# Cutting the last 4 MB store of a subject-conditioned residual matmul into six stores by partitions

## The chip, the core and the metric

One core of a Trainium2 chip runs the program. The metric is the time of one execution in device microseconds. Three timed runs of the kernel before gave 326.16, 326.69 and 326.79 us; their median, 326.69 us, is the time before.

## The reference

```python
# x: (128, 128, 1024) f32, itok: (128,) int32 in 0..7, weights: (8, 128, 128) f32
w = weights[itok]                              # one 128x128 matrix for each batch row
out = x + jnp.einsum('bct,bcd->bdt', x, w)     # (128, 128, 1024) f32
```

Each of 128 samples (128 channels by 1024 time steps, 512 KB) is multiplied by the matrix of its subject and added to itself. 67.1 MB are read and 67.1 MB are written.

## The kernel before

The identity is added to the weights on the chip, so that one matmul gives `x + w x`. The work runs over `NT` = 32 tiles of `Q` = 4 samples (2 MB). The first `FIRST` = 4 tiles have a layout of their own. A later tile lies in SBUF so that a partition holds two neighbouring channels of two samples, and the output lies in the same way.

- ACT issues all loads of `x` (`load`, `load_rows`) on its own DMA queue and copies half of each product from PSUM into `x_out` (`swap`). After each tile it writes one element of `mark`; that copy raises `s_added[1]`.
- DVE copies the other half (`copy`) and builds the next weights (`place`). The first instruction of `place` raises `s_added[0]`.
- SP issues all stores (`store`) on its DMA queue, in the order of the list `stores`: 20 stores of one tile (2 MB), then 6 stores of two tiles (`PAIR`, 4 MB). Before each it waits for `s_added[0]` and `s_added[1]`. A store reads `x_out` on 128 partitions. In a store of 4 MB a partition holds 32 KB, which goes to four places of 8 KB in `out`.
- PE multiplies in a loop, GpSimd only passes on semaphores (`s_room`, `s_ready`).

All of this stands in one block in which the waits are written by hand (`tc.tile_critical()`, L298). Only the last store is outside: `last = store(*stores[-1])` (L453) comes after that block, so SP issues it when all engines have reached the block's end. The end of the program waits for it. ACT meanwhile waits at the program's end (L449, L484) for the completion semaphores `s_out` of the stores before it.

`x_out` has eight slots, and the last store lies in two of them that no later tile needs.

## Time and profile before

| what | value |
|---|---|
| time, median of 3 runs | 326.69 us (326.16 to 326.79) |
| the profiled execution's own time | 328.88 us |
| its span, first to last instruction | 327.1 us |
| PE, DVE, ACT busy | 76%, 44%, 37% of the span |
| queue of the loads (q10), queue of the stores (q1) | 48.8%, 48.1% of 16 DMA engines |
| moved | 134.81 MB, mean 412 GB/s |

The page's line "DMA" gives the mean busy share of the 16 DMA engines in 40 slices of the span, in tenths; "GB/s" is what they moved. In a DMA view of a window, "under 512 B" counts the small packets, among which are those that raise a completion semaphore (4 bytes each). The view of a source line gives the least, median and longest duration in ns, and the first and last start in us. "SPq" and "ACTq" are the instruction queues of these engines, whose waits and DMA issues are not counted as busy.

### The profile page before, as it was taken

What the parts mean: (1) busy time and instruction counts of PE and PEld (TensorE: products, weight loads), DVE (VectorE), ACT (ScalarE), POOL (GpSimd) and SP (SyncE); (2) the same over time, 40 slices, a digit from 0 to 9 for tenths busy, and PEclk for the clock granted to TensorE, in tenths of its full rate; (3) what the DMA queues carried; (4) which work ended last, traced back from release to release, by engine and by line L of the source; (5) the groups of instructions that cost most, each with busy time, mean ns of one, the idle gap of its engine ahead of it and who ended that gap; (6) DMA issues with size and microseconds to landing.
All of it is one profiled execution on the core that took longest, in us unless ns stands there. A gap on an engine that the chain in (4) does not pass through costs nothing. (4 is left out here: it accounts for less than half of the span.)

```text
span 327.1 us, 5320 instructions
## 1 busy us (share of the span) xinstructions
PE 250.2 (76%) x1870; PEld 93.7 (29%) x1870; DVE 143.4 (44%) x207; ACT 120.4 (37%) x142; POOL 1.8 (1%) x8
## 2 busy tenths in 40 slices
PE   7899888888888888888395676978679808999200
PEld 3344333333333333333132222333223303333000
DVE  2386835555555555555513555135441530555500
ACT  0200005555555555555523555235451530555500
POOL 2000000000000000000000000000000000000000
PEclk9999979999999999999789999899898976999955
DMA  7999999999999999999999999999999999999890
GB/s 230 423 429 427 422 441 423 426 437 419 435 439 421 437 435 425 425 445 421 431 421 439 425 420 435 429 431 459 419 425 431 433 417 425 421 437 437 385 393 20
DMA packets 8247, 134.81 MB, mean 412 GB/s; under 512 B 1585, under 2 KB 2610, under 8 KB 2610
## 3 DMA queue, kind: packets, MB, share of 16 engines
q10 hardware_dynamic: 4496, 67.64, 48.8%
q1 hardware_dynamic: 3746, 67.11, 48.1%
q8 instruction: 2, 0.03, 0.0%
q14 instruction: 3, 0.02, 0.0%
HBM read 67.63 MB, written 67.11 MB: 412 GB/s over the span
## 5 line engine op out<-in xcount | busy, mean ns | idle before, releaser
L249 PE MATMUL ps<-x_in,w 64*64 64x512 f32 x1792 | 213.6, 620 | 51.1 <-PEq L240 47.4
L278 ACT COPY x_out<-ps 64x1024 f32 (+1 forms) x112 | 112.8, 1007 | 173.8 <-ACTq L293 171.7
L266 DVE COPY x_out<-ps 128x1024 f32 x56 | 68.6, 1225 | 145.7 <-DVEq L437 145.7
L249 PEld LDWEIGHTS ps<-x_in,w 64*64 64x64 f32 x1792 | 78.5, 138 | 186.2 <-issue 186.2
L197 DVE TENSOR_TENSOR w<-w_all,same 64x256 f32<-64x256 f32 x120 | 50.4, 420 | 2.6
L225 PE MATMUL ps<-x_in,w 128*128 x64 | 28.0, 597 | 1.0 <-PEq L222 1.0
L272 DVE COPY x_out<-ps 128x2048 f32<-128x2048 f32 x8 | 18.3, 2292 | 5.0 <-DVEq L426 5.0
L225 PEld LDWEIGHTS ps<-x_in,w 128*128 128x128 f32 x64 | 11.9, 190 | 17.1 <-issue 17.1
L209 DVE TENSOR_TENSOR w<-x_out 128x128 f32<-128x128 f32 x16 | 3.6, 285 | 6.4 <-DMA x_out<-in_L_cond_weights_dram 3.7
L312 PE MATMUL ps<-x_out 128*128 128x512 f32 x6 | 4.9, 982 | 1.7 <-DVE x_out L309 1.7
L284 ACT ACT_TABLE_LOAD x1 | 1.3, 1283 | 12.1 <-issue 12.1
L296 ACT COPY mark<-same 1x1 f32 (+1 forms) x28 | 5.3, 190 | 0.7
L356 PE MATMUL ps<-x_out 128*128 128x512 f32 x8 | 3.7, 601 | 0.3 <-DMA x_out<-in_L_cond_weights_dram 0.3
L312 PEld LDWEIGHTS ps<-x_out 128*128 128x128 f32 x6 | 1.8, 328 | 3.7 <-issue 2.1
L284 DVE COPY w_all<-ps 128x1024 f32<-128x1024 f32 x1 | 1.2, 1225 | 2.7 <-PE ps L356 2.7
L356 PEld LDWEIGHTS ps<-x_out 128*128 128x128 f32 x8 | 1.4, 189 | 2.7 <-issue 2.7
L284 ACT COPY w_all<-ps 128x1024 f32<-128x1024 f32 x1 | 1.0, 1012 | 0.0
L309 DVE MEMSET x_out<- 128x512 f32 x1 | 0.5, 485 | 1.0 <-SPq L298 1.0
L380 DVE TENSOR_SCALAR x_out<-x_out 1x128 int32<-1x128 int32 x1 | 0.4, 388 | 0.6 <-DMA x_out<-in_itok_B_dram 0.6
L337 POOL TENSOR_SCALAR_AFFINE_SELECT same<-same 128x256 f32<-128x256 f32 x1 | 0.5, 527 | 0.1
L325 POOL TENSOR_SCALAR_AFFINE_SELECT x_out<-x_out 128x256 f32<-128x256 f32 x1 | 0.4, 425 | 0.0
L337 POOL TENSOR_SCALAR_AFFINE_SELECT same<-x_out 128x256 f32<-128x256 f32 x1 | 0.4, 419 | 0.0
(9 smaller groups left out, 1.4 us busy)
## 6 DMA issues: line engine op xcount, KB each, us to landing
x_in<-in_x_dram ACTq DMA_DIRECT2D x56, 1024.0 KB, 12.5
out_dram<-x_out SPq DMA_DIRECT2D x20, 2048.0 KB, 56.7
out_dram<-x_out SPq DMA_DIRECT2D x6, 4096.0 KB, 46.7
x_in<-in_x_dram ACTq DMA_DIRECT2D x16, 512.0 KB, 10.0
x_out<-in_L_cond_weights_dram ACTq DMA_DIRECT2D x1, 512.0 KB, 5.2
x_out<-in_itok_B_dram SPq DMA_DIRECT2D x1, 0.5 KB
```

The source lines that it names most:

```text
L197: nc.vector.tensor_tensor(ws[u][p][h * A : (h + 1) * A], w_all[h * A : (h + 1) * A, bass.ds(subject[p * H + h], 1), :], same[h * A : (h + ...
L209: nc.vector.tensor_tensor(ws[u][q // H][:, :, q % H * D : (q % H + 1) * D], w_nat[:, bass.ds(subject[q], 1), :], eye, ALU.add,)
L225: mm = nc.tensor.matmul(ps[p][:, bank], ws[u][p][:, 0, h * D : (h + 1) * D], x_in[:, bass.ds(slot * (Q * T) + ((p * H + h) * T + t), N)], ...
L249: mm = nc.tensor.matmul(ps[p][cols, bank], ws[i % 2][p][rows, 0, r * D + e * A : r * D + (e + 1) * A], x_in[rows, at : at + N], start=r == ...
L266: return nc.vector.tensor_copy(x_out[:, bass.ds(at, T)], ps[0][:, banks].rearrange("d b n -> d (b n)"))
L272: return nc.vector.tensor_copy(x_out[:, at : at + SIZE], ps[p].rearrange("d b n -> d (b n)"))
L278: return nc.scalar.copy(x_out[h * A : (h + 1) * A, bass.ds(at + SIZE, T)], ps[1][(1 - h) * A : (2 - h) * A, banks].rearrange("d b n -> d ( ...
L284: engine(w_all.rearrange("c s (r e a) -> c r s e a", r=R, e=R)[:, r], ps[1][:, r * R : (r + 1) * R].rearrange("c g (s a e) -> c (g s) e a" ...
L296: nc.scalar.copy(mark[:, bass.ds(slot, 1)], same[:1, 0, :1]).then_inc(s_added[1], 1)
L312: nc.tensor.matmul(ps[P - 1][:, BANKS - 1], zeros[:, :D], zeros, start=True, stop=True)
L337: nc.gpsimd.affine_select(same[:, 0, :], same[:, 0, :] if h else zeros[:, : R * D], [[2 * C, R], [-2 * C, R], [-1, A]], ALU.not_equal, 1.0 ...
L356: nc.tensor.matmul(ps[1][:, r * R + g], pick[:, r], w_raw[:, g * N : (g + 1) * N], start=True, stop=True,).then_inc(s_picked, 1)
```

## The change

The last store is issued as six stores, by partitions: 0 to 111, 112 to 119, 120 to 123, 124 and 125, 126, and 127. The first five are moved into the block, behind the hand-written waits on `s_added`, and share the new semaphore `s_tail`. Only the store of partition 127 stays behind the block. ACT waits at the end for `s_tail` as well.

```diff
+TAIL = (0, 112, 120, 124, 126, 127, 128)
...
+    s_tail = tc.alloc_semaphore("s_tail")
...
-    def store(i, n):
+    def store(i, n, first=0, last=None):
         at = i % OUT * P * SIZE
+        part = slice(first, C if last is None else last)
...
-            there,
-            x_out[:, at : at + n * P * SIZE].rearrange("a (o f) -> a o f", o=1),
+            there[part],
+            x_out[part, at : at + n * P * SIZE].rearrange("a (o f) -> a o f", o=1),
...
             store(i, n).then_inc(s_out[i % OUT], DMA)
+        i, n = stores[-1]
+        nc.sync.wait_ge(s_added[0], i + n)
+        nc.sync.wait_ge(s_added[1], i + n - FIRST)
+        for first, last in zip(TAIL[:-2], TAIL[1:-1]):
+            store(i, n, first, last).then_inc(s_tail, DMA)
...
                 nc.scalar.wait_ge(s_out[i % OUT], stored[i][1])
-    last = store(*stores[-1])
+        nc.scalar.wait_ge(s_tail, DMA * (len(TAIL) - 2))
+    last = store(*stores[-1], TAIL[-2], TAIL[-1])
```

On SP, the end of the program before the change: the five earlier stores of 4 MB, the end of the block (three rows), the wait for all engines, and the last store (`out_dram` is the output, `128x4x2048` are 128 partitions of four runs of 2048 elements).

```order
L65 DMA out_dram<-x_out 128x4x2048 [waits s_added1,s_added0] x5
L291 UNCONDITIONAL_BRANCH
L298 UNCONDITIONAL_BRANCH
L298 NO_OP [waits SP_49,DVE_sequencer_49,PE_sequencer_49,SP_sequencer_49,Activation_sequencer_49,Pool_sequencer_49]
L484 UNCONDITIONAL_BRANCH
L65 DMA out_dram<-x_out 128x4x2048
L484 UNCONDITIONAL_BRANCH
```

The same place on SP after the change.

```order
L67 DMA out_dram<-x_out 128x4x2048 [waits s_added1,s_added0] x5
L67 DMA out_dram<-x_out 112x4x2048 [waits s_added1,s_added0]
L67 DMA out_dram<-x_out 8x4x2048
L67 DMA out_dram<-x_out 4x4x2048
L67 DMA out_dram<-x_out 2x4x2048
L67 DMA out_dram<-x_out 1x4x2048
L295 UNCONDITIONAL_BRANCH
L302 UNCONDITIONAL_BRANCH
L302 NO_OP [waits SP_49,DVE_sequencer_49,PE_sequencer_49,SP_sequencer_49,Activation_sequencer_49,Pool_sequencer_49]
L494 UNCONDITIONAL_BRANCH
L67 DMA out_dram<-x_out 1x4x2048
L494 UNCONDITIONAL_BRANCH
```

Five stores now stand ahead of the wait for all engines, and one partition is stored behind it.

On ACT, the end of the program before the change: the last copy of `mark`, then the rows that only wait (`s_out0`, `s_out2`, `s_out4` are earlier stores of 4 MB, the names with 49 are engines at the end of a block).

```order
L296 COPY mark<-same 1x1
L291 UNCONDITIONAL_BRANCH
L298 UNCONDITIONAL_BRANCH
L449 NO_OP [waits SP_49,SP_sequencer_49]
L484 UNCONDITIONAL_BRANCH [waits Activation_sequencer_49,Pool_sequencer_49,PE_sequencer_49,s_out4,DVE_sequencer_49,s_out2,SP_sequencer_49,s_out0,SP_49]
L449 NO_OP [waits Activation_49,Activation_sequencer_49]
L484 UNCONDITIONAL_BRANCH
```

And after it.

```order
L300 COPY mark<-same 1x1
L295 UNCONDITIONAL_BRANCH
L302 UNCONDITIONAL_BRANCH
L458 NO_OP [waits SP_49,SP_sequencer_49]
L494 UNCONDITIONAL_BRANCH [waits Pool_sequencer_49,Activation_sequencer_49,s_tail,PE_sequencer_49,s_out4,DVE_sequencer_49,s_out2,SP_sequencer_49,s_out0,SP_49]
L458 NO_OP [waits Activation_49,Activation_sequencer_49]
L494 UNCONDITIONAL_BRANCH
```

ACT's wait now takes in `s_tail`, which the first five parts of the last store raise; its other waits are the same.

## The prediction

> **What bounds the kernel now.** I read the page's DMA parts first.

> ```profile
> DMA  7999999999999999999999999999999999999890
> q10 hardware_dynamic: 4496, 67.64, 48.8%
> q1 hardware_dynamic: 3746, 67.11, 48.1%
> out_dram<-x_out SPq DMA_DIRECT2D x6, 4096.0 KB, 46.7
> ```

> The two queues together keep 16 DMA engines busy for 97% of the span: the kernel is bound by its transfers. The stores queue up (46.7 us from issue to landing for 4 MB). Nothing in the change touches the bulk of that; it works on the slices at the right end, where the digits fall to 8, 9 and 0. So I looked at the end alone: SP's issues and waits, then the windows.

> ```profile
> 306.74 0.19 ACT L296 COPY mark<-same 1x1 f32<-1x1 f32 x1
> 307.93 0.54 SPq L65 DMA_DIRECT2D out_dram<-x_out  x1
> out_dram<-x_out SPq DMA_DIRECT2D x1, 4096.0 KB, 18.2
> SPq L484 <- DMA out_dram<-x_out: 17.5, 1, 17.5
> core 0: us, PE busy (x) PEld busy (x) DVE busy (x) ACT busy (x) POOL busy (x), PEclk, DMA share, GB/s
> 308.00:309.00 1.00, 0.00 (x0) 0.00 (x0) 0.00 (x0) 0.00 (x0) 0.00 (x0) 1.00 0.31 131
> 309.00:310.00 1.00, 0.00 (x0) 0.00 (x0) 0.00 (x0) 0.00 (x0) 0.00 (x0) 0.81 1.22 524
> 310.00:315.00 5.00, 0.00 (x0) 0.00 (x0) 0.00 (x0) 0.00 (x0) 0.00 (x0) 0.50 0.98 419
> 318.80:319.50 0.70, 0.00 (x0) 0.00 (x0) 0.00 (x0) 0.00 (x0) 0.00 (x0) 0.50 0.01 0
> 319.50:326.00 6.50, 0.00 (x0) 0.00 (x0) 0.00 (x0) 0.00 (x0) 0.00 (x0) 0.50 0.06 25
> ```

> The last store is issued at 307.93 us and lands 18.2 us later, at 326.1; SP waits 17.5 us for it, and the span ends at 327.1. No compute engine works in that time. The DMA share tells more: it is about full until the window that starts at 318.8, and then 0.06 for 6.5 us. One engine of 16 is a share of 0.0625. So 15 engines are done and one works on alone. The DMA view of windows says how much is left.

> ```profile
> DMA packets 15, 0.00 MB, mean 0 GB/s; under 512 B 15, under 2 KB 15, under 8 KB 15
> DMA packets 6, 0.16 MB, mean 24 GB/s; under 512 B 1, under 2 KB 1, under 8 KB 1
> q1 hardware_dynamic: 6, 0.16, 5.7%
> DMA packets 2, 0.03 MB, mean 109 GB/s; under 512 B 1, under 2 KB 1, under 8 KB 1
> DMA packets 114, 3.70 MB, mean 407 GB/s; under 512 B 1, under 2 KB 1, under 8 KB 1
> q1 hardware_dynamic: 114, 3.70, 94.5%
> ```

> The first row is the window from 318.8 to 319.3: 15 small packets, the completions of 15 engines. The next two are 319.3 to 326.0: 6 packets, five of data and the sixteenth completion. 0.16 MB in five packets is 32 KB each, one partition of the store; 5.7% of 16 engines over 6.7 us is 6.1 us, or 1.22 us a packet. The fourth row is 315.8 to 316.1: a completion and one data packet. The late engine finishes the store before only then, while the others had begun the last one by about 309.5, and 8 packets of 1.22 us take it to 325.7. The last two rows (309.6 to 318.7) check the packet: 113 data packets in 94.5% of 16 x 9.1 us are 1.22 us each. So one engine is some 6.3 us behind, with the same 8 packets (128 partitions over 16 engines) as all others. The end is set by this engine's backlog alone.

> **The change part by part.** *Earlier issue.* The first part no longer waits for the block's end. It needs `mark`, which ends at 306.93, so it is issued near 307.0 instead of 307.93. That serves the engines that stood idle (share 0.31 in 308 to 309); the late engine has work queued until 315.96 and gains 0.

> *Six issues for one.* All stores take the same time to issue:

> ```profile
> L65 SPq DMA_DIRECT2D out_dram<-x_out x26: 538/539/637, 21.6 to 307.9; - x26
> ```

> Five extra issues are 5 x 0.54 = 2.7 us on SP, from 307.0 to 309.7; the block's end and the last issue follow until about 310.5. Between the old issue (307.93) and the rise of the share (309 to 310) lie some 1.2 us, so the last descriptors are there by 312. The cover is the first part: 7 packets of 1.22 us keep each engine busy until 316.5 at least. Cost 0; without that cover it would be up to 2.7 us. Nothing but the block's end is queued behind these issues on SP.

> *The split itself.* 112 partitions are 7 for each of 16 engines, if that store spreads as the 128 did. The other 16 partitions go out in stores of 8, 4, 2, 1 and 1. That a store of one partition can use one engine is seen at the start, in the window from 0 to 2.2:

> ```profile
> DMA packets 2, 0.00 MB, mean 0 GB/s; under 512 B 1, under 2 KB 2, under 8 KB 2
> x_out<-in_itok_B_dram SPq DMA_DIRECT2D x1, 0.5 KB
> ```

> One data packet and one completion, where the last store has 16. So what matters is how many of the 16 extra packets the late engine gets. The bounds are 0 and 5 (one from each small store): 7 to 12 packets instead of 8, -1.22 to +4.88 us. No row names the late engine. If each small store starts at the same engine, the sets are nested, and half the engines get none, four get one, two get two, one gets three and one all five. I take 0, since this is the largest group.

> [...]

> *The most loaded engine.* An on-time engine with 12 packets ends four packets later than its completion at 318.8 to 319.3: 323.7 to 324.2, less up to 0.93 us where it starts earlier. The late engine with 7 ends at 325.7 - 1.22 = 324.5. So the late one still ends last, by 0.3 us or more.

> *A longer way out.* The late engine's last packet now belongs to a store that raises `s_tail`, so ACT, not SP, hears of the end. What each does then is seen by line:

> ```profile
> L484 ACTq EVENT_SEMAPHORE  x6: 17/38/8382, 308.0 to 327.0; - x6
> L484 SPq DRAIN  x3: 7/7/7, 326.2 to 326.5; - x3
> L484 ACTq DRAIN  x2: 8/8/8, 317.0 to 326.5; - x2
> L449 ACTq EVENT_SEMAPHORE  x1: 17/17/17, 316.8 to 316.8; - x1
> ```

> ACT's long wait (8.38 us from about 308.06) ended at 316.4, when the store before landed; its other waits, the event at 316.8 and the drain at 317.0 followed, 0.6 us in all. SP's drain came at 326.2, 0.15 us after the landing at 326.1. If ACT is the last to hear, its chain costs 0.6 - 0.15 = 0.45 us more. The bounds are 0 (`s_tail` is waited for last and the rest overlaps) and 0.6; I take 0.45, since the list of ACT's waits is nearly the same as before.

> *Sum*, in the profiled execution's own time of 328.88 us: 0 + 0 - 1.22 + 0.45 = -0.77, so 328.1. The runs' median is 326.69, 2.2 us under the profiled time; -0.77 there gives 325.9.

> **The rivals.** *The late engine gets none of the extras (forecast), 325.9.* Speaks for it: half of the engines are in this group. Against it: if the untimed lag is smaller than the profiled 6.3 us (the runs are 2.2 us shorter), the engine with 12 packets becomes the bound and the gain shrinks to as little as 0. Chance 0.53 with that.

> *It gets exactly one, 327.1.* Then it has 8 packets as before, and ACT's way out is left: +0.45. This is so if the engine is one of the four in the middle of the nested sets, and also if the small stores take turns: 8 + 4 + 2 + 1 + 1 = 16, one for each engine, in which case the change doesn't relieve the late engine at all. Chance 0.28.

> *It gets two or more: slower.* The late engine is one of those at which every small store starts. Two extras give 9 packets, +1.22 + 0.45, 328.4; three give +2.44 + 0.45, 329.6; five give +4.88, 331.6 (the last is then SP's own). It decides from two extras on. For it: nothing in the trace keeps the late engine out of this group; against: only four of 16 are in it. Chance 0.19.

> **How the numbers follow.** A measurement of this kernel can tell about 0.2%, 0.65 us, from no change; the three runs spread over 0.63. The forecast is the largest case, 325.9. Its gain is only 0.1 us beyond the bound, so of its 0.53 I count 0.36 as faster (the whole range of ACT's way out, 0 to 0.6 us, leaves -0.6 to -1.2) and 0.17 as same. Of the second case's 0.28, 0.16 is same and 0.12 slower, since +0.45 plus the run-to-run spread can pass 0.65. The third is slower, 0.19. That makes 0.36, 0.33 and 0.31. The range starts at 325.3 (-1.22 without the longer way out, and 0.2 for the spread) and reaches over the second case to the first step of the third, 328.4 and 0.2 of spread: 328.6. Left out are three and five extras, about 0.1, and a little below. The likeliest case alone would be 325.3 to 326.7.

> **What would show it.** Right: the first part issued near 307.0, six issues done by 310.5; the DMA share falling in steps after 317, since engines now hold 7 to 12 packets; a single engine at the end whose last store began near 316.0 and has 7 packets, landing near 324.9; then 1.4 us to the end instead of 1.0. Wrong: the landing still at 326.1 (one extra), or later by whole steps of 1.22 us (two or more); several packets of less than 32 KB in the small stores; or an idle stretch before the small stores arrive, which would mean that the issues are not covered.

## The result and the profile after

The change makes the kernel slower: a median of 335.23 us (four runs, 333.69 to 337.45) against 326.54 us before. The ratio is 1.0272, with a 95% interval of 1.0211 to 1.0334, or 8.9 us (the two medians lie 8.7 us apart), where the forecast was 0.8 us less. The profiled execution took 335.77 us, its span 334.0 us.

The windows of the kernel after, at the end (the last two columns are the DMA share and GB/s):

```profile
core 0: us, PE busy (x) PEld busy (x) DVE busy (x) ACT busy (x) POOL busy (x), PEclk, DMA share, GB/s
310.00:315.00 5.00, 0.00 (x0) 0.00 (x0) 0.00 (x0) 0.00 (x0) 0.00 (x0) 0.50 1.00 328
315.00:318.80 3.80, 0.00 (x0) 0.00 (x0) 0.00 (x0) 0.00 (x0) 0.00 (x0) 0.50 0.99 285
318.80:322.00 3.20, 0.00 (x0) 0.00 (x0) 0.00 (x0) 0.00 (x0) 0.00 (x0) 0.50 0.21 61
326.00:332.10 6.10, 0.00 (x0) 0.00 (x0) 0.00 (x0) 0.00 (x0) 0.00 (x0) 0.50 0.06 27
```

From 310 to 315 the engines are as busy as before (1.00, before 0.98), but move 328 GB/s in place of 419. A packet counts as busy for as long as it takes, and the packets have grown longer. The window that the prediction used, 309.6 to 318.7, now reads (a view of a window counts the packets that begin in it, each with its whole length)

```profile
DMA packets 97, 2.82 MB, mean 310 GB/s; under 512 B 11, under 2 KB 11, under 8 KB 11
q1 hardware_dynamic: 97, 2.82, 98.6%
```

86 data packets in 98.6% of 16 x 9.1 us are 1.67 us each; before they were 113 of 1.22 us. The late engine is still the last. Three short windows, 322.25 to 322.4, 327.1 to 332.5 and 330.7 to 332.3, show its last steps:

```profile
DMA packets 2, 0.03 MB, mean 218 GB/s; under 512 B 1, under 2 KB 1, under 8 KB 1
DMA packets 7, 0.13 MB, mean 24 GB/s; under 512 B 3, under 2 KB 3, under 8 KB 3
DMA packets 3, 0.03 MB, mean 20 GB/s; under 512 B 2, under 2 KB 2, under 8 KB 2
```

At 322.3 there is a completion and a new packet: here the late engine ends the store before, which it ended at 315.95 in the kernel before, 6.3 us earlier. From 322.3 to 332.0 are 8 packets of 1.21 us: seven, the completion of the 112 partitions (the last row has a packet between two completions), and one of a small store. Of the three completions in the middle row, the first, at 328.06, is another engine's; from then on the late one is alone. So its own part of the last store is as long as before. It is the store *before* that has grown. Its last three packets there can be found by joining ends to starts: each begins within 0.03 us of the end of the former, and the last one ends with the completion at 322.3. These windows hold one start each: 310.99 to 311, 314.27 to 314.273 and 319.285 to 319.295.

```profile
q1 hardware_dynamic: 1, 0.03, 2032.5%
q1 hardware_dynamic: 1, 0.03, 10402.1%
q1 hardware_dynamic: 1, 0.03, 1886.2%
```

The share times 16 times the window gives 3.25, 4.99 and 3.02 us, 11.3 in all, where three packets of 1.22 us take 3.7. So 7.6 us were lost there. The way out is longer too:

```profile
L494 ACTq EVENT_SEMAPHORE  x7: 17/38/18637, 313.7 to 333.9; - x7
L494 SPq DRAIN  x3: 7/7/7, 333.0 to 333.3; - x3
L494 ACTq DRAIN  x2: 8/8/8, 333.1 to 333.3; - x2
```

ACT's wait ends near 332.4 (18.6 us from about 313.75), and the drains come 0.6 to 0.7 us later, where SP's came 0.15 us after the landing. 6.3 + 0.5 make 6.8 of the 6.9 us between the two spans. The medians lie further apart, since the profiled execution of before was 2.3 us over its median and that of after 0.5. The excess of before lies with the late engine, which in that execution was later than in others: it ended the store before at 315.95, where the run cut along the row (below) has that completion between 312.9 and 313.2, the only one from 309.6 to 314.5.

```profile
DMA packets 16, 0.12 MB, mean 410 GB/s; under 512 B 1, under 2 KB 1, under 8 KB 1
```

So an estimate for the medians is 7.6 + 0.5 = 8.1 us of the 8.7.

### The profile page after: what moved, and what is told of

Read it like the earlier page. It is cut to its first block, busy times and chain, and to the rows that moved or that the text cites. A ratio compares the mean times of both kernels' runs of the same rounds, so it can differ in the third digit from the quotient of the medians.

```text
span 334.0 us, 5327 instructions
## 1 busy us (share of the span) xinstructions
PE 250.3 (75%) x1870; PEld 93.4 (28%) x1870; DVE 143.3 (43%) x207; ACT 120.3 (36%) x142; POOL 1.8 (1%) x8
## 3 DMA queue, kind: packets, MB, share of 16 engines
q1 hardware_dynamic: 3762, 67.11, 48.1%
q10 hardware_dynamic: 4496, 67.64, 48.0%
HBM read 67.63 MB, written 67.11 MB: 403 GB/s over the span
## 6 DMA issues: line engine op xcount, KB each, us to landing
out_dram<-x_out SPq DMA_DIRECT2D x5, 4096.0 KB, 49.7
```

## The experiments

Theory 1 is a guess of mine at the cause of the longer packets (1.67 us, before 1.22), and no view shows its mechanism: partitions that lie together share a way out of SBUF (the memory on the chip that holds `x_out`), and a store that isn't spread over all 128 of them makes the engines wait for each other there. What a run can show of it is whether the length of a packet follows the partitions that are read. Theories 2 and 3 stand in the expectation that follows.

**Each store by itself.** The kernel after, with the stores in the block replaced by nine that wait for each other. Each pair in `ALONE` is the partitions read and the rows written:

```diff
+NEAR, FAR = slice(112, 120), slice(0, 32, 4)
+ALONE = (
+    (NEAR, NEAR),
+    (NEAR, FAR),
+    (FAR, NEAR),
+    (FAR, FAR),
+    (slice(0, 128, 16), slice(0, 128, 16)),
...
+        for j, _ in stores[:-1]:
+            if j >= NT - OUT:
+                nc.sync.wait_ge(s_out[j % OUT], stored[j][1])
+        for k, (part, to) in enumerate(ALONE):
+            if k:
+                nc.sync.wait_ge(s_tail, DMA * k)
+            store(i, n, part, to=to).then_inc(s_tail, DMA)
```

> The last store is preceded by eight stores of parts of it, each issued when the one before has landed and all earlier stores too, so that each runs by itself: 8 neighbouring partitions (112 to 119) to their own rows, the same 8 to rows of partitions 0, 4, ... 28, partitions 0, 4, ... 28 to the rows of 112 to 119, the same to their own rows, 8 partitions 16 apart, 4 neighbours (120 to 123), 64 partitions, 112 partitions, and then all 128 (which overwrites the two that were written crosswise). [...] Theory 2, rows of the output that lie together collide: the lengths follow the destination, 1.2 us from neighbours to distant rows and longer from distant partitions to neighbouring rows. Theory 3, the uneven load or the six issues cost the time: every packet takes 1.2 us here. The total time means nothing.

The windows around eight of the stores, in this order: neighbours to their own rows (314.5 to 320.1), neighbours to distant rows (321.3 to 326.9), distant partitions to neighbouring rows (328.2 to 329.9), 64 partitions (345 to 355.7), 112 (357 to 369.2), 128 (370.4 to 381.2), 8 partitions 16 apart (334.1 to 337) and 4 neighbours (338.3 to 343.7).

```profile
DMA packets 16, 0.26 MB, mean 47 GB/s; under 512 B 8, under 2 KB 8, under 8 KB 8
q1 hardware_dynamic: 16, 0.26, 43.9%
DMA packets 16, 0.26 MB, mean 47 GB/s; under 512 B 8, under 2 KB 8, under 8 KB 8
q1 hardware_dynamic: 16, 0.26, 43.9%
DMA packets 16, 0.26 MB, mean 154 GB/s; under 512 B 8, under 2 KB 8, under 8 KB 8
q1 hardware_dynamic: 16, 0.26, 35.9%
DMA packets 80, 2.10 MB, mean 196 GB/s; under 512 B 16, under 2 KB 16, under 8 KB 16
q1 hardware_dynamic: 80, 2.10, 95.0%
DMA packets 128, 3.67 MB, mean 301 GB/s; under 512 B 16, under 2 KB 16, under 8 KB 16
q1 hardware_dynamic: 128, 3.67, 83.8%
DMA packets 144, 4.19 MB, mean 388 GB/s; under 512 B 16, under 2 KB 16, under 8 KB 16
q1 hardware_dynamic: 144, 4.19, 90.2%
q1 hardware_dynamic: 16, 0.26, 42.0%
q1 hardware_dynamic: 8, 0.13, 22.2%
```

The share times 16 times the window, over the data packets, is the length of a packet. Eight neighbours: 0.439 x 16 x 5.6 / 8 = 4.9 us, wherever they go. Eight partitions 4 apart: 0.359 x 16 x 1.7 / 8 = 1.2 us, although they write neighbouring rows. 64 partitions: 2.5 us; 112: 1.46 us; 128: 1.22 us. In the same way 16 apart give 2.4 us and four neighbours 4.8 us. The rows written make no difference here, and packets are long without any uneven load, so theory 2 falls, and theory 3 as it stands. Of theory 1 the runs bear out that the length follows the partitions read (eight neighbours 4.9 us, eight that are 4 apart 1.2 us). What they share, if anything, no view shows, so the lengths of the other sets, the 1.46 us of 112 among them, are measured but not explained.

**The same six stores, cut along the row.**

```diff
-TAIL = (0, 112, 120, 124, 126, 127, 128)
+TAIL = (
+    ((0, 0), (3, 2048)),
+    ((3, 0), (4, 1024)),
+    ((3, 1024), (4, 1536)),
+    ((3, 1536), (4, 1792)),
+    ((3, 1792), (4, 1920)),
+    ((3, 1920), (4, 2048)),
+)
...
+            there, here = there[:, first[0] : last[0], first[1] : last[1]], here[:, first[0] : last[0], first[1] : last[1]]
```

> Six stores again, issued at the same places and with s_tail, but cut along the row: each takes all 128 partitions, 24 KB of each first, then 4, 2, 1, 0.5 and 0.5 KB. Early issue, the number of issues, the semaphore and ACT's wait stay; the cut by partitions goes. Theory 1 (shared ways out of SBUF): the late engine has its 8 x 32 KB as before and nothing collides, 326.5 to 327.3 us. Theory 3 (issues and way out): most of the 8.7 us stays, 333 or more.

326.83 us, ratio 1.0006 (0.9987 to 1.0025): the same as before. Early issue, six issues, the semaphore and ACT's wait together cost nothing that can be seen (at most 0.8 us by the interval). SP's issues did become slower when they follow each other:

```profile
L74 SPq DMA_DIRECT2D out_dram<-x_out x31: 538/539/1404, 21.5 to 312.0; - x31
L67 SPq DMA_DIRECT2D out_dram<-x_out x31: 538/539/2051, 21.7 to 313.7; - x31
```

They take up to 1.4 us here (first row), and up to 2.05 us with the change (second row), but the DMA engines were busy meanwhile (share 1.00 from 310 to 315 with the change).

**112 and 16 partitions.**

```diff
-TAIL = (0, 112, 120, 124, 126, 127, 128)
+TAIL = (0, 112, 128)
```

> Two stores of 112 and 16 partitions in place of six: every engine has 7 and 1 packets, 8 as before. Theory 1: the 112 still collide, and the 16 neighbours too; the late engine's store before is slowed as in the change, 332 to 338 us, with packets of 2 to 6 us in the last 20 us. Rival, the small stores with the uneven load of 7 to 12 packets cost the time: 326.5 to 327.5 us.

334.17 us, ratio 1.0241 (1.0203 to 1.0279). Here every engine has 8 packets, if the 16 partitions go out one to an engine (112 alone had 112 data packets and 16 completions), and nearly all of the loss remains. Uneven load isn't needed for it.

**64 and 64 partitions.**

```diff
-TAIL = (0, 112, 120, 124, 126, 127, 128)
+TAIL = (0, 64, 128)
```

> Two stores of 64 partitions, 4 packets for each engine in each. [...] Rival (the odd number 7, or the uneven load): 8 packets of 1.2 us as before, 326.5 to 327.3 us.

334.29 us, ratio 1.0245 (1.0219 to 1.0272), well above the 327.3 us at which the rival's range ends. In the window from 309.6 to 318.5 (in the first store) 54 data packets took 85.4% of 16 x 8.9 us, 2.25 us each:

```profile
DMA packets 56, 1.77 MB, mean 199 GB/s; under 512 B 2, under 2 KB 2, under 8 KB 2
q1 hardware_dynamic: 56, 1.77, 85.4%
```

Here the time is lost in another place than with the change. The late engine ended the store before at about 314.0, as without a cut by partitions, and by its packets it ended its last one at 323.97. In the window from 324 to 331.2 are 14 more completions:

```profile
DMA packets 32, 0.59 MB, mean 82 GB/s; under 512 B 14, under 2 KB 14, under 8 KB 14
```

So the other engines end last, each with 8 packets of the last store. In the window from 318.5 to 328 the 61 data packets took 91.7% of 16 x 9.5 us, 2.28 us each:

```profile
DMA packets 82, 2.00 MB, mean 210 GB/s; under 512 B 21, under 2 KB 21, under 8 KB 21
q1 hardware_dynamic: 82, 2.00, 91.7%
```

**Half and an eighth of the bytes by partitions.** One store of all 128 partitions takes the first part of every run of 8 KB, the six stores the rest (`CUT` is 1024 or 1792 of 2048 elements; the store behind the block is cut in the same way).

```diff
+        store(i, n, 0, C, 0, CUT).then_inc(s_tail, DMA)
         for first, last in zip(TAIL[:-2], TAIL[1:-1]):
-            store(i, n, first, last).then_inc(s_tail, DMA)
+            store(i, n, first, last, CUT, SIZE).then_inc(s_tail, DMA)
```

> The last store's first half of every 8 KB run goes out as one store of all 128 partitions, the second half as the six stores by partitions. Theory 1: half of the bytes collide, so about half of the 8.7 us: 329 to 332.5 us. Rival, a fixed cost of the six stores (issues, semaphores, way out): as with the change, 333.5 to 337 us.

> As with the half, but 7/8 of every run goes out with all 128 partitions, 1/8 by the six stores. Theory 1: an eighth of the bytes collide, some 1.1 us, and up to 0.5 us for ACT's way out: 326.8 to 328.2 us. Fixed cost: 333.5 to 337 us.

Half: 330.44 us, ratio 1.0109 (1.0075 to 1.0144), 3.6 us. An eighth: 327.16 us, ratio 1.0006 (0.9985 to 1.0027). So the loss isn't a fixed cost of the stores, of which there is one more than in the change: it shrinks with the bytes that are cut by partitions. It shrinks faster than they do, since an eighth of 8.9 us would be 1.1 us and the interval ends at 0.9. A store of all partitions goes first in both runs, so they don't repeat what the change does to the store before.

**Issued only when all earlier stores have landed.**

```diff
+        for j, _ in stores[:-1]:
+            if j >= NT - OUT:
+                nc.sync.wait_ge(s_out[j % OUT], stored[j][1])
         for first, last in zip(TAIL[:-2], TAIL[1:-1]):
```

> The six stores of the change, issued only when all earlier stores have landed. Theory 1: the late engine ends the store before as in the kernel before, near 316 us, since nothing else is on its way out of SBUF; then the 112 partitions take about 11.8 us alone, as in the run of each store by itself, with long packets again, and the small ones follow: the end near 332 to 337 us. Rival (the late engine is slowed by the mere number of stores on SP's queue): it ends the store before no earlier than with the change, near 322 us.

One run, 340.05 us, over the range of 332 to 337. The windows from 309.6 to 313.6 and from 309.5 to 315.4:

```profile
DMA packets 3, 0.10 MB, mean 25 GB/s; under 512 B 0, under 2 KB 0, under 8 KB 0
q1 hardware_dynamic: 3, 0.10, 5.7%
DMA packets 4, 0.10 MB, mean 17 GB/s; under 512 B 1, under 2 KB 1, under 8 KB 1
```

With nothing beside it, the late engine's packets take 1.22 us (5.7% of 16 x 4 us for three) and it ends that store before 315.4, against 322.3 with the change. So it is the stores by partitions that stretch the late engine's older work. The run is long all the same, because these stores start only at 314.2. At its end one engine runs small stores one after another, the last of them from 335.64 to 336.85, so here it isn't the late engine that ends last.

**Which engine is late, and the forecast's own case.** Three other cuts of the 16 extra partitions, one of these lines in each run (7, 6, 3; 5, 5, 6; 4, 4, 4, 4):

```diff
-TAIL = (0, 112, 120, 124, 126, 127, 128)
+TAIL = (0, 112, 119, 125, 128)
+TAIL = (0, 112, 117, 122, 128)
+TAIL = (0, 112, 116, 120, 124, 128)
```

> [...] Theory 1 (shared ways out of SBUF): the late engine has 7 packets and still ends late, since its packets of the store before are stretched by some 6 us; 331 to 337 us. The prediction's own sum (packets of 1.22 us): 325.9 us. [...]

> [...] The time by theory 1 is again 331 to 338 us.

> Stores of 112, 4, 4, 4 and 4 partitions. [...] The prediction's own sum: 325.9 us.

The last windows of the three: 7, 6, 3 (328.6 to 331.3), 5, 5, 6 (327 to 331) and 4, 4, 4, 4 (327.5 to 329).

```profile
DMA packets 5, 0.07 MB, mean 24 GB/s; under 512 B 3, under 2 KB 3, under 8 KB 3
DMA packets 6, 0.10 MB, mean 25 GB/s; under 512 B 3, under 2 KB 3, under 8 KB 3
DMA packets 2, 0.00 MB, mean 0 GB/s; under 512 B 2, under 2 KB 2, under 8 KB 2
```

With 7, 6, 3 the completion of the 112 is followed by two packets of small stores, each with its completion. So the late engine did not get the 7 packets that I had wanted for it, and the run (335.77 us, ratio 1.0274, 1.0225 to 1.0323) says nothing on the forecast's sum. With 5, 5, 6 it had three extra packets: the window holds the completion of the 112 and three packets, the last of them still running, and the whole took 334.75 us (one run). With the change it had one. No view names the engine, or shows that it is the same one each time. With 4, 4, 4, 4 it has none: of the two completions the earlier is another engine's, the later is its completion of the 112, and no data follows. This is the case that the prediction was built on, and it took 332.62 us, ratio 1.0197 (1.0133 to 1.026).

## Why the prediction was wrong

*What bounds the end*: right. One engine's backlog sets it, before and after.

*Earlier issue, six issues for one*: the cost of 0 held (the cut along the row). The working was off: the issues took up to 2.05 us each and ended near 314.6 (the last began at 313.7 and took 0.97), not 310.5. The cover I had named, until 316.5, was still long enough.

*The split itself*: the step that failed. It took 7 packets for an engine "if that store spreads as the 128 did" and gave each the 1.22 us of the store before. The number of packets was right, their length was not: 1.46 us on average for 112 partitions alone, 1.67 us in the change's end over all engines (the late engine's own eight kept 1.21). The bounds of -1.22 to +4.88 us counted only the late engine's own packets of the last store, so they left out what the last store does to a transfer that still runs. That is where three packets took 11.3 us instead of 3.7, and the late engine ended the store before 6.3 us later than in the trace of before. The case I took (no extra packet) was not the one that happened (one extra, a rival at +0.45). It was taken because the nested sets leave half of the engines without extras; that each small store starts at the same engine was a supposition, and no view shows it. With 4, 4, 4, 4 the late engine had no extra packet, and the kernel is slower by 1.3 to 2.6% all the same. The row that was read as a store of one partition at the start is a load; what it was used for, one engine for one partition, fits the packets seen: of the 48 completions that the kernel after has from 306 to 334, 16 belong to the store before and 16 to the 112 partitions, which leaves 16 for the other 16 partitions.

```profile
DMA packets 204, 5.11 MB, mean 183 GB/s; under 512 B 48, under 2 KB 48, under 8 KB 48
```

*The most loaded engine*: with the change it was not the bound. The late engine was alone from 328.1 to 332.0, where the sum left it 0.3 us. That doesn't hold for every cut: with 64 and 64 partitions, and when the store before had landed first, other engines ended last.

*A longer way out*: right, 0.5 us for the 0.45 taken.

*The rivals*: the slower one, with 0.19, was two or more extra packets, a mechanism that didn't happen. So the 0.31 given to slower in all was given for other reasons than the one that held. Its range would have ended at 331.6. None of the rivals had packets that get longer. In the list of what would prove me wrong stood smaller packets and idle stretches, not longer ones. The doubt that the lag is smaller in other executions was right: in the run cut along the row the store before ended at 313.1, not 315.95.

## What to carry to other kernels

Before a transfer is cut, ask of each piece which partitions it reads, not only how many packets each engine gets: a piece with the same bytes per engine ran at 1.46 instead of 1.22 us a packet, and eight neighbours at 4.9. Cut a store along the row and keep all 128 partitions: six such pieces cost nothing that could be seen here (326.83 us, ratio 1.0006). And carry a duration from one transfer to another only if both have the same shape and run beside the same work: here the last transfer slowed one that was still under way, whose last three packets took 11.3 us where three of 1.22 us take 3.7.

## What the runs showed of the hardware that I had not expected

```profile
L67 SPq DMA_DIRECT2D out_dram<-x_out x29: 538/539/3785, 21.5 to 310.8; - x29
```

- One engine fell behind the others (by some 6.3 us in the trace of before), and no view names it. It had one extra packet with the change, two with 7, 6, 3, three with 5, 5, 6 and none with 4, 4, 4, 4. Why it falls behind stays open.
